# A post-norm decoder layer: the order of the work where the cross-attention loop ends and the routed feed-forward begins

## The chip, the core and the metric

The kernel runs on one core of one Trainium2 chip. The core has five engines that run side by side, each with its own queue of instructions that it works through in order: PE (TensorE, matrix products and transposes into PSUM), DVE (VectorE), ACT (ScalarE), POOL (GpSimd) and SP (SyncE, which here only issues DMAs). An instruction starts when all the semaphores that it waits for have arrived and everything ahead of it on its engine has started. The metric is device time in microseconds (us); lower is better. PSUM has eight banks; in the stage that matters here four of them are a shared ring for small PE results.

## The reference

Batch 2, 1024 tokens, width 256, 16 heads of 64, a context of 77 tokens for the cross attention, a feed-forward of width 1024 that only a part of the tokens passes through. Everything is float32.

```python
x = layernorm(x + self_attention(x))             # causal, rope on q and k, 16 heads
x = layernorm(x + cross_attention(x, ctx_1024))  # 77 keys, 16 heads

weights = x @ w_r + b_r                          # one number for each token
top_vals, _ = top_k(weights, 512)                # of the 1024 tokens of a batch
selected = weights > top_vals[:, -1]
blk = gelu(x @ W1 + b1) @ W2 + b2
x = layernorm(x + where(selected, blk, x))
```

So a token that is not selected gets layernorm(2x), and a selected one layernorm(x + blk).

## The kernel before

Three stages follow each other: self attention (to about 600 us of the profiled execution), cross attention over 16 tiles of 128 tokens (eight for each batch), and the routed feed-forward. The order of PE, DVE and ACT is written out by hand, line by line, in the last two stages (`tc.manual_schedule`, L1014); each engine gets its instructions in the order in which the Python lines run. POOL's and SP's queues come out the same before and after the change.

**A tile of the loop (class `Tile_`).** `scores` (L937) makes the 16 heads' scores on PE in two halves, DVE takes their maxima and subtracts, ACT exponentiates. `weights` (L960) sums on DVE and divides on POOL. `transposes` (L968) turns the weights, 10 pieces through three ring banks `pt_p2` of 4, 4 and 2 pieces, and ACT copies each bank to `pT2`. `output` (L990) is the product with the folded values, ten steps k = 0 to 9 into one ring bank `po_cross`; DVE adds the residual (`y`, L999, which frees the bank) and a layernorm follows, whose power of -0.5 is POOL's (`rs`, L120). `output` returns `close` (L1002), which finishes the layernorm and, in `weigh` (L782), computes the tile's routing weights. A function given to `output` as `midst` is called ahead of step `when`, and what it issues goes there on each engine.

**The loop (L1059).** Step s makes the scores and weights of tile s+1, the product of tile s-1 and the transposes of tile s. What belongs to the routers is hung in at two places: `ahead` before the product, `at_end` after the step. The loop ends at s = 14; the product of tile 14 and everything of the last tile 15 but its scores and weights are written out behind it (L1071 to L1080).

**A router (one for each batch, r0 and r1).** To find the best 512 of 1024 tokens it counts, for each token, how many routing weights are at least as large. `spread` (L788) lets PE turn the weights of some tiles into rows in one ring bank `pt_r`, and a copy puts them into `every` (ACT, or DVE for the last tile). `reach(i, first, last)` (L797) is one DVE instruction: for the 128 tokens of tile i, how many of the tokens in tiles first to last-1 reach them, added to the count so far. `select` (L806) compares with 512 and begins prefix sums on DVE; `slots` (L812) ends them with two PE products and five small DVE instructions: each token's place among the kept or the skipped. `scatter` (L828) writes the eight tiles' rows to their places in DRAM, eight indirect DMAs from POOL's queue; `load` (L838) reads them back from SP's queue, kept half first, when all have landed. `turn` (L871) transposes the four kept tiles on PE into two ring banks and ACT copies them to `x2T`. `hidden(f0)` (L880) is two of the eight feature blocks of the first feed-forward product with Gelu on ACT; `layer(j)` (L895) is the second product of a kept tile, `skipped(j)` a tile that is only normalised; both end in an indirect DMA to the output, from POOL's queue.

**What sets the order at the end.** r0's part runs while r1 is still being decided: r0's `turn`, `hidden` and `layer` fill PE, and r1's counting fills DVE. r1's `turn` follows r0's four `layer`s in PE's queue (L1094 to L1096), and can't begin before r1's rows are scattered and loaded again.

Of the kernel before, what the change touches and what calls it, by code (L numbers as in the profile page):

```python
# [22 lines left out]
NT = T // P  # L23
# [11 lines left out]
def decoder_layer(  # L35
# [24 lines left out]
    V, A, G, TE = nc.vector, nc.scalar, nc.gpsimd, nc.tensor  # L60
# [31 lines left out]
    def load_wide(w, tag):  # L92

        t = wpool.tile([P, NC, INNER], F32, tag=tag, name=f"w_{tag}")
        nc.sync.dma_start(t, w.rearrange("(c p) n -> p c n", p=P))
        return t

    def load_tall(w):

        t = wpool.tile([P, NP, C], F32, tag="tall", name="w_tall")  # L100
        nc.sync.dma_start(t, w.rearrange("(c p) n -> p c n", p=P))
        return t
# [559 lines left out]
    NK = -(-HS // P)  # L662
    def pool(name, bufs, **more):
        return ctx.enter_context(tc.tile_pool(name=name, bufs=bufs, reuse_waits="tile", **more))
# [343 lines left out]
    tiles = [Tile_(b, i) for b in range(B) for i in range(NT)]  # L1008

    def reaches(r, tiles_, first, last):  # L1010
        for i in tiles_:
            r.reach(i, first, last)

    with tc.manual_schedule(engines={TE.engine, V.engine, A.engine}):  # L1014
        first = Prepare()
        k_t = first.context("k")
        first.turn()
        tiles[0].turn()
        tiles[1].turn()
        tiles[2].turn()  # L1020
        first.fold_keys(k_t)
        v_t = first.context("v")
        first.fold_values(v_t, 0)
        first.fold_values(v_t, 1, 0, NP // 2)
        for hh in range(2):
            tiles[0].scores(hh)
        first.fold_values(v_t, 1, NP // 2, NP, A.copy)
        for hh in range(2):
            tiles[0].weights(hh)
        for hh in range(2):  # L1030
            tiles[1].scores(hh)
        for hh in range(2):
            tiles[1].weights(hh)
        first.held.close()
        early.close()
        fp = pool("ffn", 2)
        f1 = pool("ffn1", 1)
        wpool = pool("weights", 1)
        w1 = load_wide(L0_ffn_W1, "wk")
        w2 = load_tall(L0_ffn_W2)  # L1040
        routers = [Router(b) for b in range(B)]
        r0, r1 = routers


        ahead = {
            5: lambda: r0.spread(0, 4), 7: lambda: r0.spread(4, 6), 8: lambda: r0.spread(6, 7),
            9: lambda: r0.spread(7, NT), 12: r0.slots, 13: lambda: r1.spread(0, 4),
        }
        at_end = {
            5: lambda: reaches(r0, (0, 1, 2), 0, 4), 6: lambda: r0.reach(3, 0, 4),  # L1050
            7: lambda: (reaches(r0, range(4), 4, 6), r0.reach(4, 0, 6)),
            8: lambda: (r0.reach(5, 0, 6), reaches(r0, range(6), 6, 7)),
            9: lambda: (reaches(r0, range(6), 7, NT), r0.reach(6, 0, NT)),
            10: lambda: (r0.reach(7, 0, NT), r0.select()),
            12: lambda: r0.scatter(0, 4, tiles[12].turned),
            13: lambda: (r0.scatter(4, NT, tiles[13].turned), r0.load(), reaches(r1, (0, 1), 0, 4)),
            14: lambda: reaches(r1, (2, 3), 0, 4),
        }
        for s in range(B * NT - 1):  # L1059
            if s > 0:  # L1060
                for hh in range(2):
                    tiles[s + 1].scores(hh)
                for hh in range(2):
                    tiles[s + 1].weights(hh)
            ahead.get(s, lambda: None)()
            close = tiles[s - 1].output() if s > 0 else None
            tiles[s].transposes(tiles[s + 3] if s + 3 < B * NT else None)
            if close:
                close()
            at_end.get(s, lambda: None)()  # L1070
        r0.turn()  # L1071
        tiles[-1].transposes()
        close = tiles[-2].output(lambda: (r1.spread(4, 6), reaches(r1, range(4), 4, 6)))
        r1.reach(4, 0, 6)
        close()
        r1.reach(5, 0, 6)
        close = tiles[-1].output(lambda: (r1.spread(6, 7), reaches(r1, range(3), 6, 7)), NK - 2)
        reaches(r1, range(3, 6), 6, 7)
        close()
        r1.reach(6, 0, 7)  # L1080
        r0.hidden(0)
        r1.spread(7, NT, V.tensor_copy)
        reaches(r1, range(7), 7, NT)
        r1.reach(7, 0, NT)
        r1.select()
        r0.hidden(2)
        r0.hidden(4, r1.slots)
        r1.scatter(0, NT)
        r0.numbers()
        r0.ready()  # L1090
        for f in [r0.skipped(j) for j in range(NK2)]:
            f()
        r0.hidden(6)
        late = [r0.layer(j) for j in range(NK2)]  # L1094
        r1.load()
        r1.turn()  # L1096
        for f in late:
            f()
        r1.numbers()
        r1.ready()  # L1100
        for f in [r1.skipped(j) for j in range(NK2)]:
            f()
        for f0 in range(0, NF, 2):
            r1.hidden(f0)
        for j in range(NK2):
            r1.layer(j)()
# [39 lines left out]
```

## Time and profile before

| what | value |
|---|---|
| runs (us) | 830.59, 837.27, 831.27; median 831.27 |
| the profiled execution | 842.25 us, of which the span from first to last instruction is 840.5 us |
| granted TensorE clock, mean over the span | 0.985 |
| busy over the span | PE 796.4 us (95%), DVE 581.4 (69%), POOL 367.6 (44%), ACT 356.6 (42%) |
| chain that ended last | PE 79%, DVE 10%, issue 4%, POOL 4%, DMA 1%, ACT 1% |
| reach, L800, share of the span on that chain | DVE 2% |
| kept<-comp, SP's four loads, issue to landing | 4.0 to 5.4 us, median 4.7 |
| comp<-x, POOL's 16 scatters | 2.9 to 5.4 us to landing, median 3.5 |

The profile is one execution on the chip, a little over 1% longer than the median of the runs; times taken from it are in its own microseconds, counted from the span's first instruction. A busy PE may still not be at its peak, and an engine's idle time only costs something where it is on the chain that ends last. The whole change lies behind 740 us.

### The profile page before, as it was taken

Reading aid. Unit: us, or ns where it says so; the run is one execution under the profiler, and the core shown is the slowest. Engines: PE = TensorE matmul, PEld = TensorE weight load, DVE = VectorE, ACT = ScalarE, POOL = GpSimd, SP = SyncE. Lnnn points to the kernel's source line nnn. Section 1 sums busy time; section 2 is a strip of 40 time slices with the busy share of each in tenths; the row PEclk is TensorE's granted clock in tenths of the full one; section 3 lists DMA queues with packets and bytes.
Section 4 is the critical chain, followed back from the end, with each engine's and each line's share of the span. In section 5 each row is a group of like instructions: output and inputs, shape, how many; then the busy total and the mean of one; then the engine's idle time right before and its main releaser. Section 6 shows DMA issues by size and latency. Waiting matters only on the chain.

```text
span 840.5 us, 26580 instructions
## 1 busy us (share of the span) xinstructions
PE 796.4 (95%) x11432; PEld 629.2 (75%) x11432; DVE 581.4 (69%) x1345; ACT 356.6 (42%) x842; POOL 367.6 (44%) x261
## 2 busy tenths in 40 slices
PE   8999999999999899999999989899999999998996
PEld 4566688888788787788787867589778888876655
DVE  2558679668668568668776796535477788876673
ACT  2545455556456455554544554200443332333220
POOL 2733554555454554463661653213032222261574
PEclk9999999999999999999999999899999999999999
DMA  5445387577468467567474585564360000011131
GB/s 176 140 135 138 117 216 181 180 197 195 128 168 205 149 187 184 172 170 183 161 195 130 150 208 161 130 188 151 132 210 1 1 1 0 1 51 51 51 101 50
DMA packets 65328, 112.32 MB, mean 134 GB/s; under 512 B 6497, under 2 KB 43707, under 8 KB 65211
## 3 DMA queue, kind: packets, MB, share of 16 engines
q1 hardware_dynamic: 54459, 72.87, 26.9%
q10 hardware_dynamic: 9216, 33.56, 18.6%
q0 software_dynamic: 1536, 4.20, 1.3%
q8 instruction: 90, 1.47, 0.8%
q14 instruction: 27, 0.22, 0.1%
HBM read 71.24 MB, written 22.59 MB: 112 GB/s over the span
## 4 chain that ended last, share of the span: by engine, by line
PE 79%; DVE 10%; issue 4%; POOL 4%; DMA 1%; ACT 1%; POOLq 0%; SPq 0%; DVEq 0%; ACTq 0%
PE po_self L410 17%; PE ps_scores L342 16%; PE pp_kq L268 13%; PE pp_v L303 7%; PE po_proj L473 5%; PE ps_cross L945 5%; PE po_cross L997 4%; DVE reach L800 2%; PE pp_h L888 2%; PE po_ffn L899 2%; DVE pT L372 2%; PE unread L244 1%; PE pt_p L977 1%; POOL e L966 1%; POOL comp L830 1%
## 5 line engine op out<-in xcount | busy, mean ns | idle before, releaser
L355 DVE CUSTOM_DVE_ANT_0 p<-ps_scores,fence 128x512 f32<-128x512 f32 (+7 forms) x256 | 179.7, 751 | 127.2 <-PE ps_scores L342 126.8
L363 ACT ACTIVATE p<-p,neg 128x768 f32<-128x768 f32 (+7 forms) x256 | 196.3, 768 | 162.5 <-DVE neg L355 160.6
L410 PE MATMUL po_self<-pT,v 32*64 32x256 f32 (+6 forms) x7808 | 160.4, 298 | 22.3 <-issue 17.5
L372 DVE STREAM_TRANSPOSE pT<-p 128x768 f32<-128x768 f32 (+7 forms) x256 | 175.8, 740 | 3.4 <-ACT p L363 1.8
L410 PEld LDWEIGHTS po_self<-pT,v 32*64 32x64 f32 x7808 | 139.1, 133 | 47.6 <-issue 36.3
L342 PE MATMUL ps_scores<-kq 64*128 64x256 f32 (+3 forms) x1056 | 151.8, 420 | 2.9 <-issue 1.3
L342 PEld LDWEIGHTS ps_scores<-kq 64*128 64x128 f32 x1056 | 95.0, 191 | 45.2 <-issue 29.8
L291 POOL TENSOR_TENSOR turned<-turned,sin 128x1024 f32<-128x1024 f32 x31 | 73.1, 2360 | 109.7 <-DMA turned<-raw 105.0
L268 PE MATMUL pp_kq<-xT,w_pair 128*128 128x256 f32 (+2 forms) x516 | 118.8, 382 | 1.3 <-ACT xT L203 0.8
L288 POOL TENSOR_TENSOR kq<-raw,cos 128x1024 f32<-128x1024 f32 x31 | 73.3, 2363 | 103.8 <-ACT raw L276 103.8
L268 PEld LDWEIGHTS pp_kq<-xT,w_pair 128*128 128x128 f32 x516 | 87.1, 191 | 25.2 <-issue 11.3
L966 POOL TENSOR_TENSOR e<-e,inv 128x616 f32<-128x616 f32 x32 | 38.2, 1215 | 113.8 <-DVE inv L965 96.1
L120 POOL TENSOR_TENSOR rs<-ve,neg_half 128x1 f32<-128x1 f32 x48 | 27.6, 577 | 113.3 <-DVE ve L118 112.1
L295 POOL TENSOR_TENSOR kq<-kq,turned 128x1024 f32<-128x1024 f32 x31 | 73.4, 2369 | 1.4
L997 PE MATMUL po_cross<-packed,pT 128*128 128x256 f32 (+1 forms) x320 | 72.5, 381 | 0.0
L945 PE MATMUL ps_cross<-wqk,x1T 128*128 128x308 f32 x256 | 69.2, 423 | 0.0
L997 PEld LDWEIGHTS po_cross<-packed,pT 128*128 128x128 f32 (+1 forms) x320 | 60.7, 192 | 8.9
L303 PEld LDWEIGHTS pp_v<-w_pair,xT 128*128 128x128 f32 x512 | 61.1, 192 | 4.0 <-issue 2.2
L303 PE MATMUL pp_v<-w_pair,xT 128*128 128x128 f32 x512 | 62.2, 275 | 0.0
L945 PEld LDWEIGHTS ps_cross<-wqk,x1T 128*128 128x128 f32 x256 | 47.4, 190 | 16.2 <-issue 0.7
L958 ACT ACTIVATE e<-e 128x616 f32<-128x616 f32 x32 | 22.9, 717 | 83.0 <-DVE e L954 83.0
L473 PE MATMUL po_proj<-wo,attnT 128*128 128x256 f32 x224 | 51.6, 381 | 1.5 <-ACT out_pair L422 1.0
(128 smaller groups left out, 830.7 us busy)
## 6 DMA issues: line engine op xcount, KB each, us to landing
v<-v_d ACTq DMA_DIRECT2D x64, 512.0 KB, 8.4
turned<-raw SPq DMA_DIRECT2D x64, 256.0 KB, 4.5
v_d<-v SPq DMA_DIRECT2D x16, 512.0 KB, 4.6
over<-inv_d SPq DMA_DIRECT2D x32, 256.0 KB, 4.7
attn_d<-out_pair SPq DMA_DIRECT2D x14, 512.0 KB, 3.8
attnT<-attn_d SPq DMA_DIRECT2D x8, 512.0 KB, 5.4
vo_d<-vo SPq DMA_DIRECT2D x2, 1232.0 KB
attnT<-attn_d SPq DMA_DIRECT2D x3, 768.0 KB, 6.5
```

Source lines behind the costliest of these rows:

```text
L268: TE.matmul(pp[:, cols], self.w[:, c, "kq".index(of), :], x_ts[self.b, n][:, c, cols], start=(c == 0), stop=(c == NC - 1),)
L288: E.tensor_tensor(self.kq[:, :, n * NB : (n + 1) * NB], self.raw[n], self.twice(cos, n), ALU.mult)
L295: E.tensor_tensor(dst, dst, self.turned[n], ALU.add)
L303: TE.matmul(pv[:, i, :], x_ts[self.b, 2 * n // NT][:, c, toks], self.w[:, c, 2, :], start=(c == 0), stop=(c == NC - 1),)
L342: TE.matmul(self.ps[j][:, cols], self.kq[rows, 1, t * P : (t + 1) * P], self.kq[rows, 0, cols.start - at : cols.stop - at], start=True, st ...
L355: V.tensor_tensor_reduce(p[:, span], self.ps[j][:, span], fence[:, T - (t + 1) * P :], -SCALE, -MASKED, ALU.add, ALU.min, neg[:, i : i + 1],)
L363: A.activation(p[:, span], p[:, span], AF.Exp, bias=neg[:, i : i + 1], scale=-1.0, accum_out=self.sums[:, j, t : t + 1],)
L372: V.transpose(p_t[:, first : first + t * step + 1 : step, :], self.p[g, j][:, span].rearrange("p (n k) -> p n k", k=P),)
L410: ins = TE.matmul(self.po[r][j * D : (j + 1) * D, n:, :], self.v4[rows, NT * k + n, j * D : (j + 1) * D], p_t[rows, first:last:step, k * R ...
L473: TE.matmul(self.po, of, wo[:, c, :], start=(c == 0), stop=(c == NP - 1))
L945: TE.matmul(ps[:, g, : Q * S], self.x_t[:, c, :], wqk[:, c, self.b, h : h + Q, :].rearrange("p h s -> p (h s)"), start=(c == 0), stop=(c = ...
L997: TE.matmul(po, self.p_t[:w, k, :], packed[self.b][:w, k, :], start=(k == 0), stop=(k == NK - 1))
```

## The change

Four things move, and nothing is added or taken out:

1. In step 13, r1's `spread(0, 4)` is no longer ahead of the product of tile 12 but inside it, ahead of its step 8 (`midst`, `NK - 2`).
2. Behind the loop, the product of tile 14 comes first, with r1's `spread(4, 6)` ahead of its step 9 (before: ahead of step 5), then the last tile's transposes, then r0's `turn`. Before, r0's `turn` was first, then the last tile's transposes, then the product of tile 14.
3. r1's spread of the last tile, its last counts and `select` go between the two feature blocks of `hidden(2)`; before, they stood ahead of `hidden(2)`.
4. r1's `slots` goes between the two blocks of `hidden(6)`, and `hidden(6)` ahead of r1's scatter and r0's skipped tiles; before, `slots` stood between the two blocks of `hidden(4)`. For DVE, POOL and SP the order stays as it was; on ACT only the copies behind the loop change places.

```diff
         ahead = {
             5: lambda: r0.spread(0, 4), 7: lambda: r0.spread(4, 6), 8: lambda: r0.spread(6, 7),
-            9: lambda: r0.spread(7, NT), 12: r0.slots, 13: lambda: r1.spread(0, 4),
+            9: lambda: r0.spread(7, NT), 12: r0.slots,
         }
...
+        midst = {13: lambda: r1.spread(0, 4)}
         for s in range(B * NT - 1):
...
-            close = tiles[s - 1].output() if s > 0 else None
+            close = tiles[s - 1].output(midst.get(s), NK - 2) if s > 0 else None
             tiles[s].transposes(tiles[s + 3] if s + 3 < B * NT else None)
...
+        close = tiles[-2].output(lambda: (r1.spread(4, 6), reaches(r1, range(4), 4, 6)), NK - 1)
+        tiles[-1].transposes()
         r0.turn()
-        tiles[-1].transposes()
-        close = tiles[-2].output(lambda: (r1.spread(4, 6), reaches(r1, range(4), 4, 6)))
         r1.reach(4, 0, 6)
         close()
         r1.reach(5, 0, 6)
...
         r1.reach(6, 0, 7)
         r0.hidden(0)
-        r1.spread(7, NT, V.tensor_copy)
-        reaches(r1, range(7), 7, NT)
-        r1.reach(7, 0, NT)
-        r1.select()
-        r0.hidden(2)
-        r0.hidden(4, r1.slots)
+
+        def last_counts():
+            r1.spread(7, NT, V.tensor_copy)
+            reaches(r1, range(7), 7, NT)
+            r1.reach(7, 0, NT)
+            r1.select()
+
+        r0.hidden(2, last_counts)
+        r0.hidden(4)
+        r0.hidden(6, r1.slots)
         r1.scatter(0, NT)
         r0.numbers()
         r0.ready()
         for f in [r0.skipped(j) for j in range(NK2)]:
             f()
-        r0.hidden(6)
         late = [r0.layer(j) for j in range(NK2)]
         r1.load()
         r1.turn()
```

## The prediction

> **What bounds the kernel now.** I read PE's timeline around the loop's end first, then the granted clock there, the chain of waits, and what PE's sequencer waited for at the turned rows. PE's timeline (start, length, instructions; in brackets its idle time before them):
>
> ```profile
> 751.57 4.48 PE L997 MATMUL po_cross<-packed,pT 128*128 128x256 f32 x20
> 755.88 1.26 PE L977 MATMUL pt_p<-ident,e 128*128 128x128 f32 x10
> 760.70 1.21 PE L877 MATMUL pt_x<-ident,kept 128*128 128x128 f32 x8 [3.56 <-DVE route L784]
> 761.70 2.34 PE L977 MATMUL pt_p<-ident,e 128*128 128x128 f32 x10
> 763.84 2.85 PE L997 MATMUL po_cross<-packed,pT 128*128 128x256 f32 x10
> 766.52 0.38 PE L794 MATMUL pt_r<-ident,route 128*128 128x128 f32 x2
> ...
> 773.41 3.60 PE L888 MATMUL pp_h<-x2T,w_wk 128*128 128x512 f32 x8
> 777.36 0.29 PE L794 MATMUL pt_r<-ident,route 128*128 128x128 f32 x1 [0.35 <-DVE route L784]
> 777.49 5.32 PE L888 MATMUL pp_h<-x2T,w_wk 128*128 128x512 f32 x12
> 782.96 0.39 PE L815 MATMUL pp_slot<-sums,ones 128*128 128x9 f32 x2 [0.16 <-DVE sums L810]
> ```
>
> PE idles 3.56 us ahead of r0's turned rows. The name in the bracket misleads: r0's load was issued at 756.53 and took 4.0 us, which is 760.5. Behind it PE runs at half speed for a while (10 transposes take 2.34 us there and 1.26 elsewhere). Granted clock, by stretches of 3.41 us (length, PE busy, clock, DMA):
>
> ```profile
> 754.65:758.06 3.41, 2.49 (x17) 1.00 0.21 41
> 758.06:761.47 3.41, 0.77 (x7) 1.00 0.88 296
> 761.47:764.89 3.42, 3.42 (x16) 0.50 0.00 0
> 764.89:768.30 3.41, 3.41 (x19) 1.00 0.00 0
> ```
>
> The chain of waits (start, length, what) shows who sets the end from there on:
>
> ```profile
> 766.94 0.38 ACT every L795
> 767.35 1.93 DVE reach L800 x8
> ...
> 778.28 0.22 DVE every L795
> 778.52 3.59 DVE reach L800 x16
> ...
> 783.61 0.18 DVE above L818
> ...
> 784.93 1.92 POOL comp L830
> ...
> 798.14 4.77 DMA out_dram<-y,rows
> ```
>
> r1's counts on DVE, then `slots`, then POOL's scatters and output writes. PE's own queue arrives at r1's turned rows (802.64) just when they do:
>
> ```profile
> L877 PEldq EVENT_SEMAPHORE  x2: 51/51/51, 760.6 to 802.5; - x2
> ```
>
> r1's kept load, issued at 798.40 with 4.1 us to landing, is there at 802.5. So two chains end together: PE's work, and counts, slots, scatter, load. Only what shortens both shortens the kernel.
>
> **Step 13's spread.** Ahead of the product, PE waited 0.67 us for tile 11's route weights (740.68 to 742.00 for 0.6 us of work). At step 8 of the product, 3.5 us on, they are there: PE gains 0.67 us and ends the loop at 756.47 instead of 757.14. Worth nothing: the product of tile 14 needs the bank that DVE's `y` of tile 13 frees at 757.39 + 0.37 = 757.76, and DVE there waited for POOL's `rs`, not PE. The copy to `every` stands behind two exponentials on ACT (745.53), later than the moved transposes end (about 745.2). Uncovered, it would cost its 0.57 us on ACT, with five to spare before its reader at 751.1.
>
> **Product ahead of transposes and turn.** A product's 20 passes take 4.32 us (0.216 each). Tile 14's now starts at 757.85, runs at the full clock over time that was idle, and reaches its spread after 18 passes: 757.85 + 3.89 = 761.74 (tile 13's weights: 760.62, no wait). From that transpose to the first count DVE needs 767.35 - 766.52 = 0.83: counts start at 762.57 instead of 767.35, 4.8 us earlier. The last tile's transposes and r0's turn follow on PE to about 764.7, the rows long loaded. The ring's banks are handed out anew, and in the built program tile 15's product takes the bank of tile 14's, so it waits for DVE's `y` behind four counts: 769.61 - 4.78 = 764.83, a new wait of 0.1 to 0.3 us. It starts at 764.9 and ends at 764.9 + 4.32 + 0.13 (spread) = 769.35, where `hidden` begins: 4.1 us earlier than 773.41. Its spread at step 8 (768.36) lets DVE go on at 769.0 instead of 773.11, so 0.7 of the 4.8 is lost to a DVE wait. On ACT the copies only change places; Gelu's table load (1.28 us) comes ahead of the first Gelu, as before.
>
> **The last counts inside hidden(2).** A `hidden` pass takes 13.84 / 32 = 0.4325 us. The spread now stands 12 passes behind the start, not 8: 769.35 + 5.19 = 774.54; DVE's copy follows its 0.29 us at 774.87. DVE could have begun at 778.19 - 4.11 = 774.08, so 0.8 us are lost; the copy is 3.3 us earlier, and select's sums end at 782.91 - 3.32 = 779.6.
>
> **Slots inside hidden(6).** Now PE's queue decides, not DVE: 16 more passes stand ahead, 774.54 + 0.13 + 6.92 = 781.59, two microseconds behind the sums. That is 1.37 us earlier than 782.96. Scatter, POOL's `rs` and output writes, and the load behind them have unchanged durations and all move by 1.37: the kept rows land at 802.51 - 1.37 = 801.14.
>
> **What is late next.** PE does the rest of `hidden(6)` (4 passes, 1.73, behind slots' 0.47) and the four layers (13.98): 781.59 + 0.47 + 1.73 + 13.98 = 797.77, 4.9 us earlier than 802.64. Then it waits 3.4 us for rows that land at 801.14. So the idle time is not removed but moved, from 757 to 798, and what ends later is worth 1.37 us so far.
>
> **The clock behind the moved wait.** The rows above: a stretch with PE 23% busy (0.77 of 3.41) is followed by one at clock 0.50. Elsewhere in this trace stretches 42, 46, 49 and 53% busy (those before 454.3, 290.4, 536.2 and 225.6) are followed by half clock, and stretches 54% busy (317.7, 502.1) are not. An idle of 3.4 us leaves some stretch of 3.41 us at least half idle wherever their edges fall, so I expect half clock behind it. There it costs: PE's r1 `hidden` runs from 803.44 without a gap to the end. One half stretch costs between 0.2 us (its edge early, most of it over the wait and the turned rows) and 1.7 us (all on products); if the stretch of the wait's end is also poorly filled, there are two, about 2.0 us. I take 1.2, the middle of that, since the edge's place is free.
>
> The Trainium skill ("TensorE: Matmul & The Clock Gate", Part 1, the table of the two states) says that the clock halves after at least one idle window of about 3.4 us and that windows run freely; read strictly, a wait of 3.4 us hardly ever fills a whole window, nothing halves, and the sum stays at -1.4 us. The trace's row differs (23 to 53% busy is enough), and I go by it.
>
> **Sum.** -1.37 + 1.2 = -0.2 us in 840.5, against the profiled execution's 842.25; carried to the runs, 831.27 - 0.2 = 831.0. Bounds: clock 0.2 to 2.0 gives -1.2 to +0.6; for slots' place, the sum of some ten rows of one execution, I allow half a microsecond either way: -1.7 to +1.1.
>
> **Rivals.**
> - *Faster, the clock stays up:* the sum is -1.4, 829.9. For it: at 802.43 a stretch 74% busy kept its clock. Against: the idle is 3.4 us, not 0.9. It would need PE to arrive 1.8 us later or the rows to land that much earlier.
> - *Faster, PE alone is the bound:* all 4.9 us come through, 826.4. It needs the rows by 797.8; POOL's eight scatters alone take from 784.93 to 795.8 and would have to start 3.4 us ahead of the place that the queue gives to `slots`. Hardly possible.
> - *Slower, half clock twice:* if an edge falls within about a microsecond after 799.4, the stretch that follows holds the rest of the wait, the two gaps of the turned rows (0.21 and 0.68 before) and half-speed work, and is followed by another. Place: 800 to 807 us; price 2.0 and half a microsecond of the turned rows' delay; -1.4 + 2.5 = +1.1, 832.4. It decides from a price over 1.4 us. For it: at 536.2 the trace has two half stretches in a row, the first 61% busy. Against: that takes about a third of the places of the edge.
> - *Slots later than before:* if `hidden` began over 1.4 us later than 769.35 (the bank wait on `y` longer than 0.3), the load would come later than now. That needs the DVE row at 762.57 to slip as much; nothing else stands there. Part of the half microsecond above.
>
> **How the numbers follow.** Forecast (kept rows 1.4 earlier, one half stretch): 0.5, 830.5 to 831.7. Half clock twice: 0.25. Clock up: 0.17. PE alone: 0.03. Something outside these places (the runs of before themselves spread from 830.59 to 837.27): 0.05. The range runs from beyond the clock-up case with its half microsecond, 829.0, to the twice-halved case with its own and a share of that spread, 833.8. A difference of 1%, 8.3 us, is about what a measurement of this kernel can tell from none; no case but the last reaches it. Faster 0.02, same 0.95, slower 0.03.
>
> **What would show it.** In the changed trace: no 3.56 us before `pt_x`, but an idle near 1.4 us before tile 14's product; `every` for tiles 12 and 13 near 762; DVE idling for the spreads of tiles 14 and 15, 0.6 and 0.8 us; `pp_slot` near 781.6 with select's sums done two microseconds before; PE idle for 3 us or more before r1's turned rows, and clock 0.5 behind that. I'm wrong if `slots` is not PE-bound, if the wait at 798 is under 1.6 us, or if the tail behind 801 isn't slowed.

## The result, and the profile after

| | before | changed |
|---|---|---|
| median of 20 runs each (us) | 837.5 (830.59 to 844.79) | 837.44 (832.24 to 844.21) |
| the profiled execution (us) | 842.25, span 840.5 | 837.83, span 836.1 |

The ratio changed to before is 1.002, 95% interval 0.9997 to 1.0042: no difference that can be told. (The ratios here and below leave out runs that came out over 1.5% above the fastest of the same kernel, so they are not the quotients of the two medians.) The forecast of a change near nothing (-0.2 us) stands; the time itself, 837.44, lies above the range of 829.0 to 833.8, and so does the median of the kernel before, which was 831.27 over the three runs at hand and is 837.5 over twenty.

The two profiled spans differ by 4.4 us although the medians of the runs don't. So executions have to be compared from a mark inside them. I use the start of DVE's `y` (L999) of tile 13, the last instruction of importance ahead of everything that moved behind the loop (only step 13's spread moved ahead of it): 757.39 in the profile before, 751.70 in the one after. From the mark to the end of the span, **the tail** in what follows, it is 840.47 - 757.39 = 83.08 us before and 836.06 - 751.70 = 84.36 after.

PE's timeline of the changed kernel, in the columns of the first one above:

```profile
752.22 4.12 PE L997 MATMUL po_cross<-packed,pT 128*128 128x256 f32 x18 [1.64 <-DVE y L999]
...
758.45 1.15 PE L877 MATMUL pt_x<-ident,kept 128*128 128x128 f32 x8 [0.37 <-ACT pT L983]
...
763.87 5.31 PE L888 MATMUL pp_h<-x2T,w_wk 128*128 128x512 f32 x12
...
769.13 7.03 PE L888 MATMUL pp_h<-x2T,w_wk 128*128 128x512 f32 x16
776.00 0.28 PE L815 MATMUL pp_slot<-sums,ones 128*128 128x9 f32 x2
...
778.16 13.98 PE L899 MATMUL po_ffn<-w_tall,hT 128*128 128x256 f32 x64
795.51 1.09 PE L877 MATMUL pt_x<-ident,kept 128*128 128x128 f32 x4 [3.37 <-DMA kept<-comp]
797.02 1.12 PE L877 MATMUL pt_x<-ident,kept 128*128 128x128 f32 x4 [0.42 <-DVE y L903]
798.81 15.60 PE L888 MATMUL pp_h<-x2T,w_wk 128*128 128x512 f32 x32 [0.67 <-ACT x2T L878]
```

The wait for r0's rows is gone, and a wait of 3.37 us for r1's has come. Behind it r1's 32 passes of `hidden` take 15.60 us where they took 14.00 before. Why, the granted clock says (length, PE busy, clock, DMA):

```profile
791.82:795.23 3.41, 0.32 (x2) 1.00 0.78 211
795.23:798.64 3.41, 2.21 (x8) 0.50 0.67 252
798.64:802.06 3.42, 3.25 (x4) 0.50 0.03 7
802.06:805.47 3.41, 3.41 (x9) 1.00 0.10 38
```

PE is 9% busy in the first stretch (0.32 of 3.41), and the two after it run at half clock. Of the 3.85 us that the loop's end gained (`hidden` at 16.02 us behind the mark before, 12.17 now) only 1.27 are left at `slots`. DVE's timeline shows where:

```profile
769.33 0.29 DVE L795 COPY every<-pt_r 128x128 f32<-128x128 f32 x1 [0.66 <-PE pt_r L794]
...
776.55 0.17 DVE L818 COPY above<-pp_slot 128x9 f32<-128x9 f32 x1 [2.50 <-PE pp_slot L816]
```

DVE has the sums at 774.05 and then waits 2.50 us for `slots`, which stands in PE's queue behind 16 passes. In the chain of waits, DVE's counts are no longer on the end's path; PE's own queue is, and then the same scatters and, as before the change, the first output write, for whose landing DVE's `y` waits:

```profile
776.55 0.18 DVE above L818
...
777.87 1.92 POOL comp L830
...
791.08 5.36 DMA out_dram<-y,rows
...
796.54 0.43 DVE y L903
```

### The profile page after: what moved, and what is told of

The parts are those of the page before. It is cut to its first block, busy times and chain, and to the rows that moved or that the text cites. A ratio compares the mean times of both kernels' runs of the same rounds, so it can differ in the third digit from the quotient of the medians.

```text
span 836.1 us, 26583 instructions
## 1 busy us (share of the span) xinstructions
PE 795.6 (95%) x11432; PEld 629.7 (75%) x11432; DVE 580.6 (69%) x1345; ACT 356.3 (43%) x842; POOL 367.6 (44%) x261
## 3 DMA queue, kind: packets, MB, share of 16 engines
HBM read 71.24 MB, written 22.59 MB: 112 GB/s over the span
## 4 chain that ended last, share of the span: by engine, by line
PE 82%; DVE 6%; POOL 4%; issue 3%; DMA 3%; ACT 1%; ACTq 0%; POOLq 0%; SPq 0%; DVEq 0%
PE po_self L410 18%; PE ps_scores L342 17%; PE pp_kq L268 14%; PE pp_v L303 7%; PE po_proj L473 5%; PE po_cross L997 5%; PE ps_cross L945 5%; PE pp_h L888 3%; DMA v<-v_d 2%; PE po_ffn L899 2%; PE unread L244 1%; POOL comp L830 1%; PE pt_p L977 1%; DVE e L954 1%; POOL e L966 1%
## 5 line engine op out<-in xcount | busy, mean ns | idle before, releaser
L410 PE MATMUL po_self<-pT,v 32*64 32x256 f32 (+6 forms) x7808 | 158.4, 297 | 19.5 <-issue 15.1
```

The costliest lines, as they stand in the source:

```text
L410: ins = TE.matmul(self.po[r][j * D : (j + 1) * D, n:, :], self.v4[rows, NT * k + n, j * D : (j + 1) * D], p_t[rows, first:last:step, k * R ...
```

## The experiments

The theory: the new order of product, transposes and turn is worth about 4 us; the later places of the last counts and of `slots` give some 2.5 of it away, and the rest goes to half clock behind the wait that this makes. The rivals are in the expectations. Every number below is from one profile of each kernel, in us behind its own mark: the starts of r0's first `hidden`, of the last of DVE's sums, of PE's products of `slots`, of r1's turned rows and of r1's `hidden`. The tail is cut in two at `slots`, since what happens ahead of it is another matter than what happens behind. Only e1 and e6 were timed in more than one run; tails of one program can lie 1.2 us apart (e8), so smaller differences between single tails say little.

| kernel | hidden | sums (start of the last) | slots | r1's turn | r1's hidden | slots to end | tail |
|---|---|---|---|---|---|---|---|
| before | 16.02 | 25.35 | 25.57 | 45.25 | 47.42 | 57.51 | 83.08 |
| changed | 12.17 | 22.18 | 24.30 | 43.81 | 47.11 | 60.06 | 84.36 |
| e8, changed again | 12.18 | 22.19 | 24.31 | 43.98 | 46.12 | 58.87 | 83.18 |
| e4, changed, PE kept busy | 12.18 | 22.18 | 24.30 | 43.84 | 46.45 | 57.81 | 82.11 |
| e3, slots sooner | 12.18 | 22.19 | 22.59 | 42.24 | 44.39 | 59.16 | 81.75 |
| e1, order alone | 12.18 | 21.44 | 21.75 | 41.24 | 44.39 | 59.99 | 81.74 |
| e6, order and buffers | 12.18 | 21.44 | 21.75 | 41.30 | 43.14 | 57.06 | 78.81 |
| e2, late places alone | 16.02 | 26.03 | 28.15 | 47.60 | 50.67 | 60.12 | 88.27 |
| e5, before, PE kept busy | 14.45 | 23.78 | 24.00 | 43.68 | 46.31 | 57.97 | 81.97 |
| e7, before, buffers | 15.22 | 24.55 | 24.78 | 44.70 | 46.55 | 57.43 | 82.21 |

**e1: the order alone.** Against the changed kernel:

```diff
-        r0.hidden(2, last_counts)
-        r0.hidden(4)
-        r0.hidden(6, r1.slots)
+        r1.spread(7, NT, V.tensor_copy)
+        reaches(r1, range(7), 7, NT)
+        r1.reach(7, 0, NT)
+        r1.select()
+        r0.hidden(2)
+        r0.hidden(4, r1.slots)
...
         for f in [r0.skipped(j) for j in range(NK2)]:
             f()
+        r0.hidden(6)
```

> The changed kernel with its first two parts alone: last counts ahead of hidden(2) and slots between the blocks of hidden(4), as before the change. I measure the tail, from DVE's start of y (L999) of tile 13 to the end of the span: 83.1 us in the kernel before, 84.4 in the changed one. Theory (PE's place for slots gave the gain of the new order away): sums ready near 21.6 us behind the mark, slots right then, 3.9 us earlier than before the change; PE and the kept rows arrive together, no idle time of 3 us before r1's turned rows and no half clock behind it; tail 79.0 to 79.6, time 0.4 to 0.5% under the kernel before. Rival (the new order itself brings nothing, the end is set elsewhere): tail 82.5 to 84.5, ratio 1.00.

Median 834.85 us over 12 runs, before 835.57 over 17 on the same chip, ratio 0.9984 (0.9958 to 1.001). Slots come 3.82 us earlier than before the change, as expected, and PE doesn't wait for the rows. But the tail is 81.74, not 79.0 to 79.6. Its PE timeline from there:

```profile
776.48 0.36 PE L815 MATMUL pp_slot<-sums,ones 128*128 128x9 f32 x2 [0.25 <-DVE sums L810]
...
797.78 0.66 PE L877 MATMUL pt_x<-ident,kept 128*128 128x128 f32 x4 [1.21 <-DVE y L903]
799.11 15.70 PE L888 MATMUL pp_h<-x2T,w_wk 128*128 128x512 f32 x32 [0.68 <-ACT x2T L878]
```

The second pair of turned rows waits 1.21 us for a bank that DVE's `y` frees, and this is DVE's timeline there:

```profile
797.30 0.42 DVE L903 TENSOR_TENSOR y<-po_ffn,plus 128x256 f32<-128x256 f32 x1 [3.64 <-DMA out_dram<-y,rows]
```

There are five buffers for these `y` (L902, L919). Four are held by r0's skipped tiles until their output writes land, so the second layer waits for the first of those writes, which takes 5.55 us to land here, beside the load of r1's rows. And the clock (same columns as above) gives the gaps their price: 1.52 of 3.41 busy, 45%, and half clock next.

```profile
795.90:799.31 3.41, 1.52 (x11) 1.00 0.53 204
799.31:802.73 3.42, 3.42 (x5) 0.50 0.03 7
```

So the rival (nothing from the order) falls and the theory is short of one link: behind the rows comes the buffer.

**e6: the same, with nine buffers for y.** At both places, L902 and L919:

```diff
-            y = fp.tile([P, C], F32, tag="yf", name="y", bufs=5)
+            y = fp.tile([P, C], F32, tag="yf", name="y", bufs=9)
```

> The changed kernel's first two parts alone, as in e1_order_only, and nine buffers instead of five for the feed-forward's rows y (L902, L919). In e1_order_only the slots were 3.84 us earlier than before the change, as expected, but r1's hidden began only 3.0 us earlier: DVE's y of r0's second layer waited 3.64 us for the first skipped tile's output write, whose buffer it takes, PE's second pair of turned rows waited 1.21 us for the bank which that y frees, and half clock followed. Theory (the buffer is the new end of the chain, and its gap brings the half clock): without it no 1.21 us gap, r1's hidden begins 43.0 to 43.3 us behind the mark (47.4 before the change), clock 1.0 in it, tail 78.6 to 79.2, ratio 0.994 to 0.996. Rival (rows, bank and writes come at the same time anyway): tail 81 or more.

Median 833.97 us over 12 runs, before 836.93 over 17, ratio 0.9958 (0.9919 to 0.9997): some 0.4% under the kernel before, with an interval that ends just short of 1. Against the changed kernel it was not timed side by side. PE's timeline:

```profile
795.79 1.06 PE L877 MATMUL pt_x<-ident,kept 128*128 128x128 f32 x8
797.64 14.00 PE L888 MATMUL pp_h<-x2T,w_wk 128*128 128x512 f32 x32 [0.78 <-ACT x2T L878]
```

The eight turned rows follow each other without a wait, `hidden` 0.78 us behind them, and its 32 passes take 14.00 again. Tail 78.81, 4.27 less than before the change and inside the expected range; 3.82 of it is the earlier `slots`. So the order is worth its 4 us once the buffers are there.

**e7: nine buffers in the kernel before.** The edit of e6 alone.

> The kernel before with nine buffers for y and nothing else. Theory (in the kernel before the buffer held PE up by 0.21 us only): tail 82.7 to 83.1. Rival (the buffer alone gives what e6_order_bufs gives): tail under 82.

The tail is 82.21, under the expected 82.7 to 83.1. But the difference stands ahead of `slots` (24.78 against 25.57), where the buffers play no part: in this execution r0's load was issued 1.24 us ahead of the mark and its rows were turned 2.71 behind it, in the other 0.86 ahead and 3.31 behind. That is 0.60 of the 0.79 us; the remaining 0.2 fit the half clock, which began 2.3 us behind the mark here and 4.1 there. From slots to the end, 57.43 against 57.51: the buffers give the kernel before 0.1 us. The rival falls: the buffers only count where the order has brought the rows forward.

**e3: slots sooner.** In the changed kernel, `slots` after `hidden(4)` instead of inside `hidden(6)`:

```diff
-        r0.hidden(6, r1.slots)
+        r1.slots()
+        r0.hidden(6)
```

> The changed kernel with slots between hidden(4) and hidden(6) instead of between the blocks of hidden(6), 4 passes of PE earlier. Theory: slots 1.7 us earlier than in the changed kernel, just behind the sums; PE's idle time before r1's turned rows shrinks from 3.4 to about 1.7 us, at the edge of what is followed by half clock; tail 80.2 at full clock, up to 82 where a stretch is halved. Rival (the clock, not the place, is the whole loss): tail 81.8 or more.

Slots 1.71 us earlier, PE's wait for the rows 1.80 instead of 3.37, one half stretch, tail 81.75. That lies on the border of what the rival expected (81.8 or more), so the tail doesn't decide between them; the rows do, which are turned 1.57 us earlier (42.24 against 43.81). PE's timeline:

```profile
798.99 0.63 PE L877 MATMUL pt_x<-ident,kept 128*128 128x128 f32 x4 [1.80 <-DMA kept<-comp]
```

The place of `slots` in PE's queue alone moves the rows, nearly one to one. e1 has them a microsecond earlier still and the same tail, because of the buffer.

**e2: the late places alone.** In the kernel before, `r0.hidden(2, last_counts)`, `r0.hidden(4)`, `r0.hidden(6, r1.slots)` as in the change, and the order behind the loop as before.

> The kernel before with the third and fourth part alone: last counts inside hidden(2), slots inside hidden(6), order of product, transposes and turn as before. Theory: slots at 28.2 us behind the mark (y of tile 13) where before it was 25.6, PE idle again for over 3 us before r1's turned rows and one or two stretches of half clock behind it; tail 85.8 without the clock, 86 to 88.4 with it. Rival (the late places cost nothing, since DVE sets slots): tail 83 to 83.5.

Slots at 28.15, a wait of 3.31 us for the rows, two half stretches, tail 88.27: 5.2 us more than before the change. PE's timeline:

```profile
798.42 0.93 PE L877 MATMUL pt_x<-ident,kept 128*128 128x128 f32 x4 [3.31 <-DMA kept<-comp]
```

This is what the third and fourth part of the change cost by themselves: `slots` 2.58 us later (28.15 against 25.57), and 2.55 later where the new order is there (24.30 against e1's 21.75). With the order's 3.82 that leaves the change's 1.27. The tails don't add up in this way, e1's being 1.34 under that of before and e2's 5.19 over it, since half clock and the wait for the buffer come on top of each.

**e4 and e5: the idle time filled.** e4 puts three products of constants, read by nobody, into the changed kernel's wait for r1's rows; e5 the same three into the kernel before, ahead of `r0.turn()`.

```diff
+        def keep_busy(n):
+            t = ps_x.tile([P, 2, NB], F32, tag="sx", name="unread2")
+            for _ in range(n):
+                TE.matmul(t[:, 0, :], ident, ident.unsqueeze(1).to_broadcast([P, NB // P, P]), start=True, stop=True)
...
         r1.load()
+        keep_busy(3)
         r1.turn()
```

> The changed kernel with three 128x512 products of constants, read by nobody, on PE between r0's layers and r1's turned rows, 2.6 us of the 3.4 that PE waits there. Theory (the idle time brings half clock, which costs 1.2 to 2.6 us): clock stays at 1.0 from there on, tail 81.8, that is 1.3 under the kernel before. Rival (the tail is slow for another reason): tail 84.0 to 84.6, products or not.

e4's PE timeline:

```profile
797.24 2.74 PE L1048 MATMUL unread<-ident 128*128 128x512 f32 x6
...
802.07 0.66 PE L877 MATMUL pt_x<-ident,kept 128*128 128x128 f32 x4 [0.65 <-DVE y L903]
803.41 14.00 PE L888 MATMUL pp_h<-x2T,w_wk 128*128 128x512 f32 x32 [0.68 <-ACT x2T L878]
```

The rows come at the same time (43.84), and with PE busy ahead of them the clock stays up and the 32 passes take 14.00: tail 82.11, 2.25 less than the changed kernel, 0.3 more than expected, since the buffer's wait is 0.65 here. So the clock cost the changed kernel about 2.25 us in its first profile, 1.60 of it in the 32 passes.

> The kernel before with three 128x512 products of constants, read by nobody, on PE ahead of r0's turned rows, 2.6 us of the 3.56 that PE idles there. Theory (the idle time costs as half clock behind it, and the counts wait for PE there): clock 1.0 around the loop's end, r0's hidden 1.7 us earlier (14.3 us behind the mark instead of 16.0), slots as much earlier, tail 81.2 to 81.9 where 83.1 was. Rival (only the order of the product matters): tail 82.9 to 83.2.

`hidden` begins at 14.45, 1.57 earlier than before, slots as much, tail 81.97, just over the expected 81.9: the turned rows wait 0.67 us for the buffer instead of 0.21. PE's timeline there:

```profile
761.54 1.25 PE L977 MATMUL pt_p<-ident,e 128*128 128x128 f32 x10
```

The ten transposes take 1.25 us again, not 2.34. Of the 3.85 us that the new order brings `hidden` forward (16.02 to 12.17), 1.57 can so be had without a new order, by keeping the clock up; the other 2.3 come with the order.

**e8: the changed kernel once more.**

> The changed kernel unchanged, for a second profile of its end. Theory (the half clock behind r1's turned rows depends on where free-running stretches of 3.41 us begin): slots at 24.3 us behind the mark to within 0.1, half clock for one or two stretches behind the wait, tail between 82.2 and 84.8, not the same as the first profile's 84.4 unless the stretches fall alike. Rival (a fixed loss): tail 84.3 to 84.4 again.

Every mark up to r1's turn is the same to within 0.2 us, the wait is 3.54, and only one stretch is halved, from 45.6 behind the mark: tail 83.18. The clock there (same columns as above):

```profile
796.03:799.44 3.41, 1.69 (x8) 1.00 0.25 42
799.44:802.85 3.41, 1.28 (x8) 1.00 1.07 387
802.85:806.27 3.42, 2.88 (x4) 0.50 0.12 41
```

The wait is split between two stretches, 50% and 38% busy, and only the second is followed by half clock. PE's timeline at r1's `hidden`, 15.41 us where the first profile has 15.60:

```profile
803.39 15.41 PE L888 MATMUL pp_h<-x2T,w_wk 128*128 128x512 f32 x32 [0.68 <-ACT x2T L878]
```

The same program has tails 1.2 us apart, in the main by where the stretches fall.

## Why the prediction was right on the change and wrong on the time

**Wrong: the level.** The step that failed is "carried to the runs, 831.27 - 0.2 = 831.0", and with it the range's upper end of 833.8. Three runs, two of them at 831, were taken for the kernel's time, with "a share of that spread" for the third at 837.27. Twenty runs of the same kernel, these three among them, have their median at 837.5, and the two at 831 are the lowest of all: the level was read from an unlucky draw, and nothing in the change moved it. The profiled execution of before, 842.25 us, was a fourth run and a warning; I took it for the same time a little longer, and it lies within the twenty, with four above it. Where runs differ, ten profiles show: the cross attention's first score step (DVE L954) starts at 601.0 to 608.4 us, and from there to its last it takes 146.38 to 146.44 us in every one of them. So the spread of some 7 us is made ahead of this step, where the self attention runs, and ahead of everything that changed. PE's busy time up to it (stretch, length, busy, clock, DMA), in the kernel before and in e7, whose self attention is the same and which gets there 7.4 us earlier:

```profile
0.00:608.43 608.43, 578.24 (x10435) 0.99 0.60 166
```

```profile
0.00:601.04 601.04, 572.49 (x10434) 0.99 0.61 165
```

Of the 7.4 us, 5.75 are busy time and 1.64 idle time. The busy time goes with the half clock: over the ten profiles it is 572.5 us with two half-clock stretches of 3.41 us up to there (e7), about 576 with four, 577.0 to 578.2 with five (before and changed among them), 578.8 with seven and 580.0 with eight. The idle time varies beside it, from 25.8 to 32.3 us: the profile after has as many half stretches as that of before and starts the loop 5.7 us earlier, 4.4 of it by less idle time. No experiment was made on the stage, so what sets either of them is open.

**Right: the place of slots sets the end.** Slots were put 1.37 us earlier than before and came 25.57 - 24.30 = 1.27 earlier, "two microseconds behind the sums" as DVE's wait of 2.50 shows. The steps to it, in us behind the mark, predicted and measured: tile 14's product 0.46 and 0.52; first count 5.2 and 5.3; `hidden` 12.0 and 12.2; DVE's last spread 17.5 and 17.6. The one step that went otherwise is small: tile 15's product started at 7.74, not 7.5, and without the forecast wait for the bank that `y` frees; it follows the turned rows, which waited 0.37 us for ACT. e3 and e2 show that the place of `slots` moves the rows nearly one to one. The kept rows are one branch behind `slots`, though; in the chains of both kernels the one that ends last is the first output write.

**Right: the idle time moved and brought half clock along.** Predicted 3.4 us ahead of r1's turned rows, measured 3.37. e4 shows that the half clock is due to it and that without it the tail is 82.1.

**Mis-sized: the clock's price.** I took 1.2 us from 0.2 to 2.0, whose middle is 1.1; against e4's tail it was 2.25 in the first profile (two stretches, the case that had 0.25) and 1.07 in the second (83.18 - 82.11, one stretch). The second is too low, since the turned rows waited 0.17 us for the buffer there and 0.65 in e4: the 32 passes alone took 1.41 longer. The changed tail is 1.3 and 0.1 us over the tail before, where -0.2 was forecast and -1.7 to +1.1 allowed, so the first lies just outside; the runs' ratio, with its interval from -0.3 to +3.5 us, fits both. So "no difference" in the runs doesn't confirm the -0.2; it would have come out so at +1 too. The tail of before isn't fixed either: in e7, where r0's rows came 0.6 us sooner, it is 0.9 less, and the buffers give only 0.1 of that.

**Missed: the buffer.** The prediction let everything behind the scatters move with them. The rows did; DVE's wait for the first output write did not quite: from the write's issue to its landing it was 4.8 us before, 5.4 in the changed kernel and 5.6 in e1, where write and load are issued within 0.1 us of each other. In the change this is worth some 0.3 us (e4: 0.97 under before instead of 1.27), in e1 it held r1's `hidden` up by 1.25 us (44.39 against e6's 43.14) and brought the half clock back.

**Step 13's spread** is worth nothing in the trace: PE waits 1.64 us for `y` of tile 13, which comes at its old time (148.93 us behind the first score step, 148.96 before). It wasn't tried alone.

## What to carry to other kernels

When work is moved into an idle gap, ask what PE will wait for next, and whether an instruction that a serial chain hangs on (here the two small products of `slots`) is put behind bulk work in the same queue: its place in the queue is then the chain's clock. An idle stretch costs twice on PE, as time and as half clock behind it, so a gap of this kind on the path is worth filling, even with work that nobody reads: 1.1 us of the tail in e5, 1.1 and 2.25 in e4 against the two profiles of the changed kernel, though no run times were compared. In e3 a wait of 1.8 us was enough, with the two small gaps of the turned rows behind it (1.46 of 3.41 us busy). And before a time is forecast, take the level from all executions at hand, the profiled one included; for a change of a few microseconds in a late stage, compare profiles from a mark ahead of it: `slots` of the changed kernel repeats to 0.01 us behind the mark (24.30, 24.31, 24.30) where the runs spread over 14. The mark has its limits: in the kernel before, r0's rows are still under way there, and `slots` came at 25.57 and in e7 at 24.78.

## What the runs showed of the hardware that was not expected

- A stretch that itself runs at half clock is followed by another although PE is 65% busy in it (795.23 above), where at full clock 54% was enough to keep the clock (the prediction's row at 317.7). No share is a sharp border, though: e8's stretch at full clock from 796.03 was 50% busy and kept it, its stretch at half clock from 802.85 was 84% busy and brought the clock back, and one of e4 (101.85 to 105.26), fully busy at half clock, did not.
- A write of 128 rows to the output that lands in 2.4 us (median before) took 4.8 to 5.6 beside the load of the kept rows. It goes with the order of the two issues: 4.77 to 4.84 us where the write was issued at least 0.24 us ahead of the load (before, e3, e8), 5.10 to 5.36 where it was 0.09 to 0.15 ahead (e2, e4, the changed kernel), 5.55 where it came 0.09 behind (e1). That the load is the reason was not tried alone.
